# Two cross-attention layers on one core: the values of layer 0 one product later on the tensor engine

## The chip, the cores and the metric

The kernel runs on one core of a Trainium2 chip. The time is the device time of one execution in microseconds. Three runs of the kernel before gave a median of 1915.06 us (1913.88 to 1915.12).

## The reference, cut to what matters

Two attention layers follow each other on 4 batches of 1024 tokens of width 1024, with a context of only 64 tokens for each batch. All is in float32.

```python
# layer 0: 32 query heads of 32, 8 key heads, additive mask, residual, layer norm
q = x @ Wq + bq;  k = ctx @ Wk + bk;  v = ctx @ Wv + bv
attn = softmax(q k^T / sqrt(32) + mask)          # per head, over 64 keys
x1 = layernorm((attn v) @ Wo + bo + x) * gamma + beta
# layer 1: 16 heads of 64 over layernorm(ctx), boolean mask, gated residual
y = x1 + tanh(gate) * (softmax((x1 @ Wq.T) (a @ Wk.T)^T / 8) (a @ Wv.T)) @ Wo.T
```

## The kernel before

**Blocks, subtiles, pairs.** The 4096 tokens are cut into 4 blocks of 1024, 32 subtiles of 128 (numbered t = 0 to 31) and 16 pairs of subtiles. Large products are made by a scheme with seven half-size products in place of eight (the names S1 to S4, T1 to T3, X, V, W belong to it); sums of operands for it are made on VectorE.

**The stages.** (1) Up to some 230 us: the context's keys and values, and the queries of block 0. (2) From some 230 to 600 us: `mix(t)` (L771) interleaves the attention of layer 0 of subtile t with the query products of the next block, which come out of a generator `work` (L962). (3) From some 600 to 717 us: the last 8 subtiles are mixed with `folded_queries` (L887), small products that fold layer 1's query weights with its keys (called heads below), and at the end with four steps of the first output product. (4) From then on the output product of layer 0 and all of layer 1, pair by pair. Stages 2 and 3 are what the change touches.

**One subtile of layer 0.** `attend0` (L654) makes the scores in two fronts (L680): 8 small TensorE products each into a PSUM tile `big`, which VectorE copies out with the mask added (L684). VectorE takes the maxima (L691); ScalarE takes the exponentials: 24 of the 32 heads one by one (L698), each with its sum, the other 8 together (L706), while VectorE subtracts and sums for those (L694, L711). Then VectorE inverts the sums (L712) and divides (L715) in two halves, `divide(1)` and `divide(0)`. For t below 19 (`by_turning`) the probabilities are transposed through DRAM: GpSimd's queue writes them out (L735, `p<-s`) and reads them back by quarters (L739, four transfers `pq<-p`, one buffer), and VectorE turns them with two stream transposes (L419) into two tiles `pT`; this is called the flip. From t = 19 on TensorE transposes (L407) and ScalarE copies out (L410 and L414). The **values** of a subtile (L759) are 16 small products of `pT` with the value matrix, shown as x16 by the trace; they need both flips. ScalarE copies their PSUM tile to `oT` (L398, L400) and issues its DMA (L765). For t below 19 values use the pool `big`, of two buffers, which the fronts use too; later values, heads, ScalarE's transposes and the query products share the pool `wx`, of four banks.

**The order.** `mix(t)` issues front 0, a place for other work, front 1, maxima and exponentials, a second and a third place, then the values of subtile t-2 (from t = 20 on those of t-1, whose flip is issued a little earlier), total and divide of half 1, a fourth place, the flip of t-1, total and divide of half 0, the transfers of the flip of t, and a fifth place. `other()` fills a place with one step of `work` as long as the subtile's count lasts. The count is 3 at even and 4 at odd t up to 15 and from 24 on, and 3 from 16 to 23, so that **the fourth place holds a step only at odd t up to 15 and at t = 25, 27, 29, 31**, and the fifth never holds one. In stage 2 a step is a product of queries, four matrix products of 128x512 (x8 in the trace, L576); in stage 3 it is one group of heads (L897, x8), or at t = 30 and 31 a product with Wo (L446). The layer that records the program may move instructions within an engine's list where data allow it, so an engine's list follows this order only roughly; each engine then works its own list in order.

**What waits on what around it.** Half 1's total and division do not depend on the values. The flip of t-1 writes into the two `pT` tiles that the values of t-2 read. The `big` buffer that the values fill is taken again by front 1 of subtile t+1, so ScalarE has to have copied it out by then. ScalarE's copy of `oT` stands among the exponentials of subtile t in its list.

Of the kernel before, what the change touches and what calls it, by code (L numbers as in the profile page):

```python
# [71 lines left out]
def tile_two_cross_attentions(  # L72
# [150 lines left out]
    for i in range(2):  # L223
        t = scratch.tile([P, H], F32, tag="cnat", name=f"ctx_{i}", bufs=2)
# [3 lines left out]
    for w, n in ((wk0, "wk0"), (wv0, "wv0")):  # L228
        t = wpool.tile([P, KC, 256], F32, tag="wb", name=n)
# [408 lines left out]
    def by_turning(t):  # L638


        return t < NSUB - SUB - 5
# [3 lines left out]
    def load_queries(t):  # L645
        q = qpool.tile([P, KC, P], F32, tag="q", name=f"q0_{t}")
        nc.sync.dma_start(out=q, in_=qTd[t // SUB][:, :, sub_ap(t % SUB)])

        m = small.tile([P, 2, S], F32, tag="m0", name=f"m0_{t}", bufs=2)
        for e in range(2):  # L650
            nc.sync.dma_start(out=m[:, e], in_=mask0[sub_ap(t), :])
        queries[t] = q, m
# [75 lines left out]
    def outputs0(t):  # L728

        b = t * P // L  # L730
        s = probs.pop(t)
        pTs = {}
        if by_turning(t):

            nc.gpsimd.dma_start(out=p0[t], in_=s)  # L735
            pq = pqpool.tile([P, NQ, 512], F32, tag="pq", name=f"pq0_{t}")
            v = p0[t].rearrange("(u i) (a w) -> a i u w", i=Q, a=NQ)
            for a in range(NQ):
                nc.gpsimd.dma_start(out=pq[a * Q : (a + 1) * Q], in_=v[a])  # L739

        def flip(c):
            pT = pTs[c] = ppool.tile([P, 8, P], F32, tag="pT", name=f"pT0_{t}_{c}")
            if by_turning(t):
                turn_quarters(pq, pT, (c * 8, (c + 1) * 8))
                return

            turn(s[:, c * 1024 : (c + 1) * 1024], pT, t >= NSUB - SUB)

        def values():
            oT = opool.tile([P, KC, P], F32, tag="oT", name=f"oT0_{t}")  # L750
            ps = big() if by_turning(t) else [wx(), wx()]


            for c in range(2):
                for i in range(2):
                    for e in range(2):
                        bank = ps[:, e * 512 : (e + 1) * 512] if by_turning(t) else ps[e]
                        on, at = slice(e * S, (e + 1) * S), (2 * c + i) * 32
                        nc.tensor.matmul(  # L759
                            bank[at : at + 32], v0[on, b, c, i, :],  # L760
                            pTs[c][on, i * 4 : (i + 1) * 4].rearrange("p g l -> p (g l)"),
                            start=True, stop=True, tile_position=(e * S, at),
                        )
            copy_out(oT.rearrange("p g l -> p (g l)"), ps)
            nc.scalar.dma_start(out=oTd[t // 2][:, :, sub_ap(t % 2)], in_=oT)  # L765

        return flip, values

    turned = {}

    def mix(t, count):  # L771


        front, largest, exps, total, divide = attend0(t)
        places = 5

        def other():
            nonlocal count, places
            for _ in range(-(-count // places)):
                next(work)  # L780
                count -= 1
            places -= 1

        def powers(n):
            for _ in range(n):
                if exps:
                    exps.pop(0)()

        def values(u):
            if u in turned:  # L790
                turned.pop(u)[1]()

        def flip(u):
            for c in range(2):
                turned[u][0](c)

        front(0)
        if (t + 1) % SUB:
            load_queries(t + 1)
        other()  # L800
        front(1)
        largest(0)
        powers(1)
        largest(1)
        powers(1)
        other()
        plain = t and not by_turning(t - 1)
        if plain and t - 2 not in turned:
            flip(t - 1)
        powers(1)  # L810
        other()
        powers(2)
        if t - 2 in turned:
            values(t - 2)
            if plain:
                flip(t - 1)
        total(1)
        divide(1)
        if plain:
            values(t - 1)  # L820
        other()
        if t and not plain:
            flip(t - 1)
        powers(len(exps))
        total(0)
        divide(0)
        turned[t] = outputs0(t)
        other()
# [195 lines left out]
    for t in range(last):  # L1024
        n = 28 - AHEAD if t // SUB == NBLK - 2 else 28
        mix(t, (t % SUB + 1) * n // SUB - t % SUB * n // SUB)
    go_on(FOLD_AHEAD)
    n = 4 * KC - FOLD_AHEAD + FIRST
    for i in range(SUB):
        mix(last + i, (i + 1) * n // SUB - i * n // SUB)  # L1030
# [38 lines left out]
    def turn_x1(pair, xq, pool=None, tag="xT"):  # L1069

        xT = (pool or xTpool).tile([P, KC, 2 * P], F32, tag=tag, name=f"xT_{pair}")

        def half(h):
            turn_quarters(xq, xT[:, h * HK : (h + 1) * HK, :], (h * HK, (h + 1) * HK))

        def blocks():
            lefts[pair] = left_out(xT, lpool if pool else lxpool, f"x_{pair}")

        return [lambda: half(0), lambda: half(1), blocks]
# [4 lines left out]
    flip, values = turned.pop(NSUB - 1)  # L1084
# [13 lines left out]
    for pair in range(1, NPAIR):  # L1098
# [30 lines left out]
        if pair == NPAIR - 2:  # L1129
            xq = load_x1(0)  # L1130
            turned = turn_x1(0, xq, o2pool, "o2")
# [165 lines left out]
```

## Time and profile before

| what | us |
|---|---|
| median of 3 runs | 1915.06 |
| the profiled execution | 1915.11 |
| its span on the core | 1913.3 |
| TensorE (PE) busy in the span | 1868.9 |
| VectorE (DVE) busy | 1292.1 |
| ScalarE (ACT) busy | 427.9 |
| GpSimd (POOL) busy | 179.1 |
| PE busy from 230 to 545 us (315 us) | 308.53 |
| PE busy from 600 to 720 us (120 us) | 106.05 |
| PE busy from 1200 to 1800 us, each 100 us | 100.00 |

The profile describes one execution, from the first instruction to the last. A table of stretches gives the busy time of each engine in a window, with the clock that TensorE was granted (1.00 is full) and the share of the DMA engines' time in use. A timeline row has the start, the length, the engine, the line, the operation, its output and input, the number of merged instructions, and in brackets how long the engine had stood idle before it and what released it. A matmul that has begun counts as busy, even where the next instruction of its merged row waits; so a row that is longer than its kind hides a wait too.

### The profile page before, as it was taken

The numbers are of one execution on the slowest core, as the hardware profiler recorded it, in microseconds if no ns is written. First come the engines' busy times: TensorE is split into PE (matmuls) and PEld (weight loads), VectorE is DVE, ScalarE is ACT, GpSimd is POOL, SyncE is SP. The second block draws the span as 40 slices with busy tenths as digits, with TensorE's granted clock in tenths as the row PEclk, the third lists the DMA queues.
The fourth block names the chain that finished last, engine by engine and source line by source line (L and its number), as shares of the span: only waits on it lengthen the run. The fifth ranks groups of instructions, "written<-read, shape, count | busy, mean of one in ns | idle before, by whom it ended". The sixth has DMA issues, their size and how long they took to land.

```text
span 1913.3 us, 17522 instructions
## 1 busy us (share of the span) xinstructions
PE 1868.9 (98%) x6096; PEld 880.0 (46%) x6096; DVE 1292.1 (68%) x1582; ACT 427.9 (22%) x1396; POOL 179.1 (9%) x212
## 2 busy tenths in 40 slices
PE   8999999999998899999999999999999999999999
PEld 7744444444455653343344444444444444444444
DVE  3425589789878985575568778557665766576653
ACT  1101575666536751212100001000000000000000
POOL 0016011111100103121113100000000000000000
PEclk9999999999999899999999999999999999999999
DMA  8996599899878966567473363466656565657421
GB/s 276 184 222 192 158 253 247 253 252 261 252 186 275 302 234 207 188 207 238 164 218 138 121 141 90 110 165 158 150 143 165 150 158 143 165 142 165 121 88 44
DMA packets 220745, 350.54 MB, mean 183 GB/s; under 512 B 26992, under 2 KB 146160, under 8 KB 215664
## 3 DMA queue, kind: packets, MB, share of 16 engines
q1 hardware_dynamic: 152896, 242.44, 45.8%
q0 software_dynamic: 15216, 60.83, 10.5%
q10 hardware_dynamic: 52544, 46.14, 8.8%
q8 instruction: 48, 0.79, 0.2%
q14 instruction: 41, 0.34, 0.1%
HBM read 207.53 MB, written 141.82 MB: 183 GB/s over the span
## 4 chain that ended last, share of the span: by engine, by line
PE 82%; DVE 8%; DMA 5%; issue 2%; ACT 2%; POOL 0%; SPq 0%; DVEq 0%; POOLq 0%; ACTq 0%
PE wx L446 59%; PE wx L576 14%; PE big L680 2%; DMA pq<-p 2%; PE big L924 1%; PE wx L379 1%; PE big L379 1%; DVE s L684 1%; PE big L759 1%; DMA p<-s 1%; DMA q<-qTd 1%; DVE s L715 1%; DVE mx L691 1%; DVE sm L711 1%; DMA o<-oTd 1%
## 5 line engine op out<-in xcount | busy, mean ns | idle before, releaser
L455 DVE TENSOR_TENSOR r<-wx,r 128x512 f32<-128x512 f32 x224 | 153.5, 686 | 230.1 <-PE wx L446 215.3
L698 ACT ACTIVATE s<-s,mx 128x64 f32<-128x64 f32 x488 | 162.8, 335 | 74.9 <-DVE mx L691 70.7
L502 ACT ACTIVATE s<-s 128x1024 f32<-128x1024 f32 x32 | 33.7, 1057 | 651.7 <-DVE s L501 651.7
L459 DVE TENSOR_TENSOR s<-wx,key_bias 128x512 f32<-128x512 f32 x64 | 44.1, 690 | 136.7 <-PE wx L446 136.7
L446 PE MATMUL wx<-wo_B,S 128*128 128x512 f32 x256 | 117.1, 600 | 1.5 <-DVE r L455 1.5
L576 PE MATMUL wx<-xT,wq_S 128*128 128x512 f32 x256 | 116.5, 598 | 0.8 <-ACT z L587 0.8
L446 PE MATMUL wx<-b_B,pT 128*128 128x512 f32 x256 | 115.8, 593 | 0.6 <-ACT pT L414 0.6
L446 PE MATMUL wx<-b_B,S_p 128*128 128x512 f32 x256 | 116.0, 596 | 0.0
L446 PE MATMUL wx<-a_B,xT 128*128 128x512 f32 x256 | 115.4, 592 | 0.0
L446 PE MATMUL wx<-a_B,S_x 128*128 128x512 f32 x256 | 115.3, 593 | 0.1
L576 PE MATMUL wx<-xB,wq_A 128*128 128x512 f32 x256 | 115.1, 597 | 0.0
L446 PE MATMUL wx<-wo_B,o 128*128 128x512 f32 x256 | 114.8, 596 | 0.0
L958 POOL TENSOR_TENSOR r<-r,bo 128x1024 f32<-128x1024 f32 x30 | 78.5, 2625 | 313.8 <-DMA r<-in_x_dram 159.4
L684 DVE TENSOR_TENSOR s<-big,m 128x1024 f32<-128x1024 f32 x64 | 77.4, 1215 | 28.4 <-PE big L680 26.8
L680 PEld LDWEIGHTS big<-kv,q 64*128 64x128 f32 x1024 | 71.1, 195 | 48.3 <-issue 39.9
L698 ACT ACTIVATION_READ_ACCUMULATOR s<-s,mx 128x1 f32 x488 | 91.4, 187 | 0.0
L680 PE MATMUL big<-kv,q 64*128 64x128 f32 x1024 | 82.6, 292 | 2.6 <-DMA q<-qTd 2.6
L419 DVE STREAM_TRANSPOSE pT<-pq 128x1024 f32<-128x1024 f32 x66 | 78.0, 1219 | 3.3 <-DMA pq<-p 3.3
L446 PEld LDWEIGHTS wx<-wo_B,S 128*128 128x128 f32 x256 | 47.1, 190 | 67.7 <-issue 51.2
L715 DVE TENSOR_TENSOR s<-s,sm 128x1024 f32<-128x1024 f32 x64 | 77.0, 1216 | 0.9
L446 PEld LDWEIGHTS wx<-wo_B,o 128*128 128x128 f32 x256 | 47.8, 190 | 63.5 <-issue 62.3
L446 PEld LDWEIGHTS wx<-a_B,S_x 128*128 128x128 f32 x256 | 48.5, 190 | 62.0 <-issue 58.4
(162 smaller groups left out, 2903.5 us busy)
## 6 DMA issues: line engine op xcount, KB each, us to landing
p<-s POOLq DMA_DIRECT2D x19, 1024.0 KB, 8.1
pq<-p POOLq DMA_DIRECT2D x76, 256.0 KB, 6.0
xq<-in_x_dram SPq DMA_DIRECT2D x64, 256.0 KB, 10.2
q<-qTd SPq DMA_DIRECT2D x32, 512.0 KB, 7.4
oTd<-oT ACTq DMA_DIRECT2D x32, 512.0 KB, 7.4
ad<-a POOLq DMA_DIRECT2D x16, 1024.0 KB, 8.9
o<-oTd SPq DMA_DIRECT2D x16, 1024.0 KB, 5.1
r<-in_x_dram SPq DMA_DIRECT2D x32, 512.0 KB, 5.3
```

Source lines behind the costliest of these rows:

```text
L379: nc.tensor.matmul(ps[:, 0:256], w[k // HK, c // HK][:, k % HK, sub_ap(c % HK)], ct[:, k, :], start=(k == 0), stop=(k == KC - 1),)
L419: return nc.vector.transpose(dst.rearrange("p k (u i) -> p k u i", i=Q), t[:, :, k0 * Q : k1 * Q].rearrange("p u (k j) -> p k u j", j=Q),)
L446: nc.tensor.matmul(banks[name], a[s][:, k, :], w[m][:, k, :], start=first and k == 0, stop=last and k == HK - 1, skip_group_check=True,)
L455: nc.vector.tensor_tensor(at, bank, at, ALU.add)
L459: nc.vector.tensor_tensor(at, bank.rearrange("p (h s) -> p h s", s=S), bias.unsqueeze(1).to_broadcast([P, 512 // S, S]), ALU.add,)
L502: nc.scalar.activation(s, s, AF.Exp)
L576: nc.tensor.matmul(bank, w_q[a][:, k, sub_ap(i)], rows[b][:, k, :], start=first and k == 0, stop=last and k == HK - 1, skip_group_check=True,)
L680: nc.tensor.matmul(ps[:, at : at + P], q[on, c * 4 + g, :], k0bd[on, b, c, :], start=True, stop=True,)
L684: nc.vector.tensor_tensor(quarters[:, :, c * 8 : (c + 1) * 8], ps.rearrange("p (k a l) -> p a k l", a=NQ, l=Q), mask.rearrange("p e (h l) ...
L698: nc.scalar.activation(heads[:, e, k], heads[:, e, k], AF.Exp, bias=mx[:, e, k : k + 1], accum_out=sm[:, e, k : k + 1],)
L715: nc.vector.tensor_tensor(heads[:, e], heads[:, e], wide(sm[:, e]), ALU.mult)
L958: nc.gpsimd.tensor_tensor(ru, ru, bo_sb, ALU.add)
```

## The change

The values of subtile t-2 (or t-1) are issued after the fourth place and no longer before total and divide of half 1; these, and the step of the fourth place, now come first. Only at t = 20, where two sets of values fall together, does one of them stay in front.

```diff
         powers(2)
-        if t - 2 in turned:
+        late = t - 2 in turned
+        if late and plain:
             values(t - 2)
-            if plain:
-                flip(t - 1)
+            flip(t - 1)
         total(1)
         divide(1)
+        other()
         if plain:
             values(t - 1)
-        other()
+        elif late:
+            values(t - 2)
         if t and not plain:
             flip(t - 1)
         powers(len(exps))
```

In the built program the lists differ from those before in the following. **PE:** at t = 3, 5, 7, 9, 11, 13 and 15 the values stand behind a whole product of queries that they stood in front of, or in the middle of; at t = 25, 27 and 29 behind one more group of heads and some products of the next front; at t = 31 behind one product with Wo, and the last subtile's TensorE transposes, which stood half in front of and half behind the next such product, stand together behind it. At all other t nothing moves on PE. **ACT:** at the odd t up to 15 the copy to `oT` stands behind 5 to 8 more exponentials (one to six at t = 15), mostly behind all of them; at t = 25, 27 and 29 behind two more copies of heads. **DVE:** a few neighbours change places at t = 5, 9, 13 and 15 (at 5 and 13 the last division comes in front of the turning of some input rows). **SP and POOL:** the same order.

## The prediction

> **What bounds the kernel now.** I read first the page's busy times, then the table of stretches, then the waits of PE in stage 2, then PE's and DVE's timelines. All durations are from the profiled execution, 1915.11 us with a span of 1913.3 (1.8 us lie around it); it stands 0.05 us above the median of 1915.06, so the sum is made against 1915.1.
>
> ```profile
> PE 1868.9 (98%) x6096; PEld 880.0 (46%) x6096; DVE 1292.1 (68%) x1582; ACT 427.9 (22%) x1396; POOL 179.1 (9%) x212
> ```
>
> TensorE is the bound: 98% busy. What an edit can gain is the time in which PE stands or drags: 44 us in all, and by the table of stretches these lie in few places.
>
> ```profile
> 286.80:325.40 38.60, 35.39 (x168) 15.38 (x168) 38.06 (x37) 21.12 (x101) 5.49 (x10) 0.96 0.98 256
> 325.40:389.00 63.60, 63.60 (x298) 29.27 (x290) 48.77 (x56) 43.82 (x214) 11.00 (x20) 1.00 0.89 256
> 389.00:420.90 31.90, 31.81 (x153) 14.47 (x152) 26.78 (x32) 22.11 (x107) 5.48 (x10) 1.00 1.00 257
> 420.90:459.00 38.10, 35.81 (x166) 15.50 (x170) 37.67 (x36) 22.42 (x110) 5.49 (x10) 1.00 0.88 250
> 600.00:720.00 120.00, 106.05 (x771) 71.34 (x768) 102.43 (x115) 77.61 (x181) 9.03 (x12) 0.93 0.86 290
> ```
>
> The columns after the window are its length and the busy times of PE, PE's loads, DVE, ACT and POOL, then PE's clock and the DMA share. The reader is to see two stretches of stage 2 in which DVE is full, 38.06 of 38.60 and 37.67 of 38.10 us (it turns and sums the input rows of the next block there), and PE loses 3.2 and 2.3 us; between them DVE has a quarter of its time free and PE loses nothing visible. In stage 3 PE loses most. What PE waits for in stage 2 is one thing:
>
> ```profile
> PE big L759 <- DVE pT L419: 6.2, 5, 2.1
> ```
>
> that is, the values for their flips, 6.2 us in 5 waits. The timeline shows them, and more than them: values without a wait take 1.09 us (first row below), and where the second flip comes later than the first, the row is longer by the wait inside it.
>
> ```profile
> 272.18 1.09 PE L759 MATMUL big<-pT,kv 64*32 64x512 f32 x16
> ...
> 282.55 3.60 PE L576 MATMUL wx<-xT,wq_S 128*128 128x512 f32 x8
> 288.24 2.96 PE L759 MATMUL big<-pT,kv 64*32 64x512 f32 x16 [2.09 <-DVE pT L419]
> 291.13 3.95 PE L576 MATMUL wx<-xT,wq_A 128*128 128x512 f32 x8
> ```
> ```profile
> 307.89 1.35 PE L759 MATMUL big<-pT,kv 64*32 64x512 f32 x16
> ...
> 323.89 2.10 PE L759 MATMUL big<-pT,kv 64*32 64x512 f32 x16 [1.78 <-DVE pT L419]
> 325.92 3.70 PE L576 MATMUL wx<-xB,wq_A 128*128 128x512 f32 x8
> ```
>
> **Part 1, stage 2: values behind one product (3.6 us) at odd t.** The wait before plus the row's excess over 1.09 is, at t = 3, 5, 7, 9, 11, 13, 15: 0.77 (row of 1.86 at 253.9), 2.09 + 1.87 = 3.96, 1.78 + 1.01 = 2.79, 0.70 (1.79 at 356.3), 0, 1.47 + 1.01 = 2.48 (422.3) and 0.48 + 1.01 = 1.49 (457.6). Together 12.2 us. A product that stands ready runs in that time; each sum is near or below 3.6 us, so at the place itself all of it goes. That is the upper bound of the gain. What decides is the next subtile, where no product moves. PE then asks for the flip of t-1 earlier; does it come earlier? The flips of subtiles 3, 4 and 5 on DVE:
>
> ```profile
> 286.85 2.37 DVE L419 STREAM_TRANSPOSE pT<-pq 128x1024 f32<-128x1024 f32 x2 [2.37 <-DMA pq<-p]
> ...
> 305.76 2.36 DVE L419 STREAM_TRANSPOSE pT<-pq 128x1024 f32<-128x1024 f32 x2
> ...
> 322.51 2.36 DVE L419 STREAM_TRANSPOSE pT<-pq 128x1024 f32<-128x1024 f32 x2
> ```
>
> The first waits for its DMA, not for PE; after it DVE has no gap but 0.42 us until 324.8. So at **t = 5** the 3.96 are gained and at **t = 6** they are given back: PE, earlier by 0.77 + 3.96, has done its products at 304.4 (in the old run's times; the last of them still waits for a DVE addition at about 300.8), while the second flip ends at about 307.6 against 308.1 before. Values of 4 end at about 308.4 in place of 309.2. I keep 0.77 up to here. At **t = 7** the flip of 5 stays where DVE puts it, 322.5 to 324.9; the moved product fills that time, the values run at 325.1 without a wait, and the 2.79 are kept, if the following stretch lets PE be ahead: there DVE is 77% busy and waits itself for PE (1.27 and 1.22 us for the fronts of subtile 8), so it follows. At **t = 9** 0.70 more is kept. At **t = 13** the same as at 5 happens: the flip of 11 waits 0.89 us for its DMA, then DVE is full to 459, so the 2.48 come back as a wait at **t = 14** (its values already wait 0.43 + 1.01). At **t = 15** 1.49 are kept, since the full stretch ends there. Sum kept: 0.77 + 2.79 + 0.70 + 1.49 = 5.75.
>
> **Covers.** ScalarE's copy to `oT` now stands behind up to 8 more exponentials of 0.33 us, 2.7 us. It has to be done by front 1 of the next subtile, which stands 4.8 us behind the end of the values (a front of 1.1, a product of 3.6). At t = 5 the exponentials would end at 291.3, the copy (0.99) at 292.3, front 1 stands at 295.5: hidden. At t = 7 it is tight, 330.6 against 331. If the cover is gone, at most 2.7 us less what PE gained. In return ScalarE no longer stands in front of the copy, 11.4 us in 5 times before, with exponentials queued behind it. The flip of t-1 needs the values of t-2 done; DVE comes to it some 15 us later, so nothing. The divisions ahead of the values: the same DVE work in nearly the same list, 0; at t = 5 and 13 the division of half 0 is some 1 us earlier and a front's copy 1 us later, which I set against each other. SP's and POOL's lists keep their order; 0.
>
> **Part 2, stage 3: values behind one more group of heads.** At t = 25:
>
> ```profile
> 620.83 1.13 PE L897 MATMUL wx<-kT,wq1T 64*128 64x256 f32 x4 [0.47 <-ACT pT L410]
> 621.88 1.09 PE L759 MATMUL wx<-pT,kv 64*32 64x512 f32 x16
> 622.90 0.49 PE L680 MATMUL big<-kv,q 64*128 64x128 f32 x4
> 623.96 1.40 PE L897 MATMUL wx<-kT,wq1T 64*128 64x256 f32 x7 [0.57 <-ACT a L903]
> ```
>
> Here values start at once, and the group behind them waits 0.57 us for a bank that ScalarE frees at L903. The banks go round: with the order changed, the moved group finds its banks free, and it is the values that need the two banks of the group before, both copied out only at 624.4, behind an exponential of 1.8 us. PE then has 1.06 (heads) + 0.4 (fronts) to do from 621.9, stands some 1.0 us in place of 0.57, and reaches the next transposes some 0.3 us later. DVE sets the pace of these subtiles (some 11.9 us each, of which 11.4 are DVE work), so the true cost lies between 0 and 0.45; I take 0.3 each for t = 25 and 29. At t = 27 DVE stands 1.40 us for the load of `o` and adds four sums of 0.7; PE has time, 0. At t = 31 the transposes of the last subtile stand together: the second half needs banks that the copies of the first half (0.5 each) free, between 0 and 1.1 us; nearest is one copy with its start-up, 0.7. Part 2 costs 1.3, with bounds of 0 and 2.5.
>
> **Sum.** 1915.1 - 5.75 + 1.3 = **1910.7 us**, 0.23% under the median. By the bounds: from 1902.9 (all of 12.2, nothing lost) upwards.
>
> **The clock.** Where PE has stood long, it then drags. The group of heads that takes 1.06 us took 1.98 at 612.9, and a front of 1.09 took 1.74 at 614.6, after waits of 2.05 and 2.55 us; 1.6 us were lost in one such stretch. At 288.2, after 2.09 us, the same shows (values 2.96, then a product of 3.95 in place of 3.70), after 1.78 us at 323.9 it does not. The limit lies near 2 us in this trace. [...]
>
> **Rivals.** *All of the waits go* (1915.1 - 12.2 + 1.3 = 1904.2): DVE's full stretches would have to start earlier with PE. For it: they start at a DMA whose chain starts at a division that PE's fronts release. Against it: the DMA share of 0.96 (230 to 286.8 us) and 1.00 ahead of them, and that inside them DVE has nothing to give. *DVE or the DMA chain sets the pace throughout*: each wait comes back one subtile later, the gains are nil, and stage 3 costs up to 1.3: 1915.1 to 1916.4. For it: DVE is at 85% over stage 2, and each flip hangs on two DMAs with 8 us and 6 us to landing. Against it: no wait for values at t = 8, 10, 12. *The clock* (slower): the wait returned at t = 6 and t = 14 is 2.1 us or more, and those of about 1 us in stage 3 join others there; from some 2 us in a stretch on, each brings 1.6 us of half clock. Four such, 6.4, with 1.3 of part 2, and only the gains at t = 3, 9 and 15 left (2.96, if the drag eats those of t = 7): 1915.1 + 6.4 + 1.3 - 2.96 = 1919.8. Against it: the old run has one such stretch in stage 2, which the change removes from t = 5. That the change does nothing is excluded for 11 of 32 subtiles by the lists.
>
> **Chances.** Forecast 0.45 (1908.5 to 1912.7), all waits 0.17, no gain 0.20, clock 0.18. A measurement of this kernel can tell some 0.2% from no change, 3.8 us: 1911.2 is the border, two thirds of the forecast's case lie below it. Faster 0.17 + 0.33 = 0.50; same 0.12 + 0.18 = 0.30; slower 0.18 + 0.02 = 0.20. The range that leaves out 2 in 10 takes in the middle of the first rival and all of the second and stops short of most of the third: 1904.0 to 1917.5.
>
> **What would show it.** Right: no wait in front of the values at t = 5, 7, 13, 15; PE at its front of subtile 8 some 3.5 us earlier than at 330.4; waits of 2 us or more at the values of t = 6 and 14. Wrong: the values of t = 7 wait in spite of the product (then DVE runs later than I hold); front 1 waits for the copy to `oT`; PE's clock below 0.96 in the two full stretches, or below 0.93 from 600 to 720; stage 3 longer by more than 2.5 us.

## The result, and the profile after

The changed kernel takes 1909.5 us (median of 8 runs, 1906.8 to 1911.4), the kernel before 1913.8 us beside it (8 runs, 1911.8 to 1915.6): ratio 0.9974, with a 95% interval of 0.9966 to 0.9983 (the two medians alone, divided, give 0.9977). Run once more with other kernels (e11 below) the ratio is 0.9959 (0.9943 to 0.9974). The forecast, 1910.7 of 1915.1, is a ratio of 0.9977. The gain is 0.26%, more than the 0.2% that can be told from no change, though the first interval reaches down to 0.17%.

The profiled execution took 1911.4 us with a span of 1909.7, 3.6 us less than before. The busy times:

```profile
PE 1865.5 (98%) x6096; PEld 879.6 (46%) x6096; DVE 1290.2 (68%) x1582; ACT 427.4 (22%) x1396; POOL 178.5 (9%) x212
```

The counts of instructions are the same, and TensorE is the bound as before. What PE waits for from 230 to 545 us:

```profile
PE big L759 <- DVE pT L419: 4.1, 2, 2.1
PE wx L576 <- DVE u L593: 1.1, 2, 0.8
PE big L680 <- DMA q<-qTd: 0.4, 1, 0.4
```

Five waits for flips have become two, and two kinds have come that the old list did not have. PE's timeline from t = 5 to t = 8 shows where (start, length, operation, and in brackets the idle time ahead of it with what ended it):

```profile
284.58 3.60 PE L576 MATMUL wx<-xT,wq_A 128*128 128x512 f32 x8
288.11 1.09 PE L759 MATMUL big<-pT,kv 64*32 64x512 f32 x16
...
299.40 3.70 PE L576 MATMUL wx<-xN,wq_A 128*128 128x512 f32 x8 [0.76 <-DVE u L593]
305.23 2.10 PE L759 MATMUL big<-pT,kv 64*32 64x512 f32 x16 [2.13 <-DVE pT L419]
...
313.07 10.57 PE L576 MATMUL wx<-xB,wq_A 128*128 128x512 f32 x24
323.57 1.09 PE L759 MATMUL big<-pT,kv 64*32 64x512 f32 x16
324.59 1.12 PE L576 MATMUL wx<-xT,wq_S 128*128 128x512 f32 x2
326.13 1.16 PE L680 MATMUL big<-kv,q 64*128 64x128 f32 x16 [0.41 <-DMA q<-qTd]
```

At t = 5 and t = 7 the values (288.11 and 323.57) stand behind the product and start at once, in 1.09 us. At t = 6 they wait 2.13 us, and their row is 2.10 long because the second flip comes late too. The front of t = 8, at 330.41 before, comes at 326.13, after a wait of 0.41 us for its own load. The flips of subtiles 3, 4 and 5 on VectorE:

```profile
285.49 2.37 DVE L419 STREAM_TRANSPOSE pT<-pq 128x1024 f32<-128x1024 f32 x2 [2.42 <-DMA pq<-p]
...
303.85 2.36 DVE L419 STREAM_TRANSPOSE pT<-pq 128x1024 f32<-128x1024 f32 x2
...
320.60 2.36 DVE L419 STREAM_TRANSPOSE pT<-pq 128x1024 f32<-128x1024 f32 x2
```

They start 1.4, 1.9 and 1.9 us earlier than before: VectorE's full stretch follows its first load, not PE, which is 5.9 us ahead at the front of t = 6. In the table of stretches (length, busy PE, PEld, DVE, ACT, POOL, PE's clock, DMA share, GB/s) VectorE is still full in the first of these rows:

```profile
286.80:325.40 38.60, 35.71 (x174) 15.41 (x172) 38.09 (x38) 21.41 (x105) 6.70 (x13) 1.00 0.96 254
...
420.90:459.00 38.10, 35.76 (x165) 16.11 (x162) 37.15 (x37) 22.52 (x105) 5.88 (x12) 1.00 0.88 273
600.00:720.00 120.00, 105.80 (x730) 68.49 (x730) 100.26 (x114) 74.44 (x171) 11.26 (x13) 0.91 0.84 285
```

Where the time came from, by the same instructions' starts in the two profiles (us, gained at the place; a minus is given back):

| at t = | 3 | 5 | 6 | 7 | 8 | 9 | 10 to 12 | 13 | 14 | 15 | to the end of stage 2 | sum |
|---|---|---|---|---|---|---|---|---|---|---|---|---|
| forecast | 0.77 | 3.96 | -3.96 | 2.79 | 0 | 0.70 | 0 | 2.48 | -2.48 | 1.49 | 0 | 5.75 |
| measured | 0.97 | 4.49 | -3.98 | 2.37 | -1.02 | 0.90 | 0.19 | 2.75 | -2.17 | 1.75 | -0.12 | 6.13 |

The row at t = 7 includes the wait of 0.41 us in front of t = 8; the 1.02 at t = 8 are the row of its values, 2.10 us long in place of 1.09. PE enters stage 2 0.4 us earlier, which is scatter, leaves it 6.6 us earlier and is still 6.4 us ahead at the last values of stage 3. Some 3 us of that go near 717 us. PE, VectorE and GpSimd there:

```profile
720.14 5.40 PE L446 MATMUL wx<-wo_T,S 128*128 128x512 f32 x8 [2.24 <-DVE r L455]
```
```profile
719.39 0.69 DVE L455 TENSOR_TENSOR r<-wx,r 128x512 f32<-128x512 f32 x1 [3.07 <-POOL r L962]
```
```profile
717.02 6.95 POOL L962 TENSOR_TENSOR r<-r,bo 128x1024 f32<-128x1024 f32 x3 [34.03 <-DMA r<-in_x_dram]
```

GpSimd adds `bo` to rows that have just landed, VectorE's addition waits for it, PE waits 2.24 us for VectorE (0.97 before) and then needs 5.40 us for a product of 3.70. Whether that belongs to the change is a question for the runs.

### The profile page after: what moved, and what is told of

Its sections match the earlier page's. It is cut to its first block, busy times and chain, and to the rows that moved or that the text cites. A ratio compares the mean times of both kernels' runs of the same rounds, so it can differ in the third digit from the quotient of the medians.

```text
span 1909.7 us, 17518 instructions
## 1 busy us (share of the span) xinstructions
PE 1865.5 (98%) x6096; PEld 879.6 (46%) x6096; DVE 1290.2 (68%) x1582; ACT 427.4 (22%) x1396; POOL 178.5 (9%) x212
## 4 chain that ended last, share of the span: by engine, by line
PE 80%; DVE 9%; DMA 5%; ACT 3%; issue 2%; POOL 0%; SPq 0%; DVEq 0%; ACTq 0%; POOLq 0%
PE wx L446 59%; PE wx L576 12%; ACT s L698 2%; PE big L680 2%; DVE s L684 2%; PE wx L379 1%; PE big L379 1%; PE big L928 1%; DVE mx L691 1%; DVE s L715 1%; DMA q<-qTd 1%; DMA pq<-p 1%; DMA p<-s 1%; PE big L759 1%; DVE sm L711 1%
## 5 line engine op out<-in xcount | busy, mean ns | idle before, releaser
L299 ACT ACTIVATE rstd<-rstd 128x1 f32<-128x1 f32 x32 | 6.5, 203 | 316.1 <-DVE rstd L298 316.1
```

## The experiments

**Theory.** A product in front of the values fills the wait at odd t; where VectorE's full stretch goes on, the next subtile hands the gain back; stage 3 costs little. **Rivals:** the gain comes from elsewhere (stage 3, the divisions); or what hands the gain back is not VectorE's work but the loads.

### Which stage: e1 and e2

e1 keeps the old order from t = 20 on, e2 keeps it up to t = 19. Against the changed kernel, e1 reads

```diff
-        other()
         if plain:
             values(t - 1)
-        elif late:
+        other()
+        if late and not plain:
             values(t - 2)
```
For e1 was expected:

> The values one product later up to t = 19 only, stage 3 as before. My theory (the gain is PE's removed waits for flips in stage 2, and stage 3 costs or brings nearly nothing): 3.5 to 5.5 us under the kernel before, as the whole change. Rival (the gain, or a loss that hides a larger one, lies in stage 3 or in where the slow-clock stretches fall there): less than 2 or more than 6.5 us under it.

and for e2:

> The values later at t = 25, 27, 29, 31 only. My theory: within 1.5 us of the kernel before (I had priced it at +1.3; the changed kernel's trace shows PE no later at the end of stage 3 than at its start). Rival: 3 us or more under it.

e1: 1909.0 us, ratio 0.9973 (0.9963 to 0.9983). e2: 1915.9 us, 1.0005 (0.9996 to 1.0014). The whole gain is stage 2's; stage 3 costs 1.0 us, with an interval of -0.8 to 2.7, so it cannot be told from nothing.

### Which subtiles: e3 and e4

e3 moves the values only at t = 5 and 13, the places said to be handed back; e4 at all the others of stage 2. The edit is `moved = t in (5, 13)`, or the rest, added to the condition.

> The values later at t = 5 and 13 only, the two places with the longest waits (3.96 and 2.48 us), where VectorE is full behind them. My theory: the time gained there is given back one subtile later, so 0 to 1.5 us under the kernel before, with PE some 4 us ahead at the front of subtile 6 and less than 1 us ahead at the front of subtile 7. Rival (what counts is the sum of waits removed, wherever): 6.4 of 12.2 us removed, so half of the whole change or more, 2.5 us and more under it.

> The values later at t = 3, 7, 9, 11 and 15, not at 5 and 13 and not in stage 3. My theory: 3.5 to 5.5 us under the kernel before, all that the whole change brings, though only 5.75 of 12.2 us of waits are removed. Rival (the sum of waits counts): half of the whole change, 2 to 2.5 us under it.

e3: 1912.7 us, 0.9988 (0.9979 to 0.9997); e4: 1909.8 us, 0.9977 (0.9963 to 0.9990). In e3 6.4 us of waits go at t = 5 and 13, and the waits at t = 6 and 14 stand there at 2.12 and 2.00 us; 1.5 us are left in its profile between the values of 0 and of 18, and 4.4 in e4's, of 6.1 in the changed kernel's. By the ratio e3 gains 2.3 us (0.6 to 4.0), between what the theory and the rival allowed it. So t = 5 and 13 are mostly returned, not wholly, and the other five places carry most of the gain.

### The divisions: e5

Moving the two divisions ahead of the values, without the product, was not run: in the built program it leaves the lists of all five engines as they were. e5 asks the other half: the product alone.

```diff
-        total(1)
-        divide(1)
         other()
         if plain:
             values(t - 1)
         elif late:
             values(t - 2)
+        total(1)
+        divide(1)
```

> The product stands in front of the moved values as in the changed kernel, but the divisions stand behind the values again. With the old order of the product, moving the divisions alone leaves the instruction list of every engine as it was, so the question is only whether they matter beside the moved product. Theory (the time comes from the product alone, and VectorE divides at its own pace): the values of t = 5, 7, 13, 15 start without a wait, the waits at t = 6 and 14 are 2.0 to 2.2 us, and the time is that of the changed kernel, 1909.5 us, within 1.5; ratio to before 0.997 to 0.9985. Rival (the divisions in front are what keeps the quotients early enough for the next subtile): the waits at the flips or fronts behind grow by 1 us at five to ten places, 1913 to 1916 us, ratio 0.9995 to 1.001.

e5: 1910.2 us, 0.9982 (0.9973 to 0.9990). The waits at t = 6 and 14 are 2.13 and 1.71 us as the theory has it, but two rows differ: at t = 5 the row of the values is 1.96 long, and at t = 16 they wait 1.87 us. In the traces the lists of e5 and of the changed kernel differ in stage 2 only on VectorE, near 255 us (t = 3) and from 385 to 393 us (t = 11), so no other order stands directly behind those two rows; at t = 16 a wait of 0.51 us stands in e4 too. The intervals overlap with the changed kernel's, so whether the divisions in front are worth about a microsecond beside the product stays open.

### What hands the gain back: e6, e9, e12

e6 lets the last three of the four sums over the next block's rows (2.27 us each on VectorE) run in the first steps of the next block, e9 puts the second sum (L184) on GpSimd:

```diff
-            run(sums[1:])
+            if not spread:
+                run(sums[1:])
...
-            fills = {}
+            fills = dict(enumerate(later))
```
```diff
+        def tt(out, a, b, op, n):
+            return (nc.gpsimd if n in moved else nc.vector).tensor_tensor(out, a, b, op)
...
-                rows, fills = rows0(blk + 1)
+                rows, fills = rows0(blk + 1, (1,))
```

> The changed kernel, and the last three of VectorE's sums over the next block's input rows run in the first three steps of the next block, not at the end of the old one's; so VectorE's full stretches (near t = 4 to 6 and t = 12 to 14) lose some 8 us of work. Theory (a full VectorE is what hands the waits on from t = 5 to 6 and from 13 to 14): the waits at t = 6 and 14 fall from 2.13 and 2.00 us to under 0.7, with them the slow stretch of the values' row goes (2.10 us back to near 1.1), and stage 2 ends 1.5 to 4 us earlier than in the changed kernel: 1905.5 to 1908 us, ratio 0.9955 to 0.997. Rival (the flips there hang on their loads, not on VectorE): the waits stay at 1.8 us or more, and the sums are merely late for the next block's first products: 1909 to 1913 us, ratio 0.9975 to 0.9995.

> The changed kernel, and the second of the four sums over the next block's input rows (L184, 2.27 us on VectorE, in front of the flip that the values at t = 6 and t = 14 wait for) runs on GpSimd. Theory (VectorE's amount of work in the full stretch hands the waits on to t = 6 and 14): that flip comes 2.3 us earlier, the wait of 2.13 us at t = 6 falls under 0.3 us and that of 2.00 us at t = 14 likewise, and the time falls by 1 to 4 us under the changed kernel's: ratio to before 0.9955 to 0.997. Rival (the sum of about 6.5 us on GpSimd delays the loads that GpSimd issues for the flips, or slows VectorE beside it): the wait at t = 6 stays at 1.5 us or more or comes back at t = 7 or t = 8, ratio 0.9975 to 1.001.

e6: 1919.5 us, 1.0026 (1.0014 to 1.0038); e9: 1919.1 us, 1.0019 (1.0006 to 1.0031). Both are slower than the kernel before. The sum that e9 moved takes 4.54 us on GpSimd there (at 299.64 us), where 6.5 was expected, an estimate (GpSimd's additions of half that width take 2.34 to 3.34 us in the changed kernel); VectorE's rows beside it, a front's copy of 1.20 and a flip of 2.36 us, are as long as in the changed kernel (1.21 and 2.36). PE's waits in stage 2 of e6:

```profile
PE big L681 <- DMA q<-qTd: 8.1, 1, 8.1
PE big L760 <- DVE pT L419: 3.7, 3, 2.5
PE wx L577 <- DVE u L594: 0.9, 1, 0.9
```

The wait at t = 6 did fall, from 2.13 to 1.06 us (1.05 in e9), though not under the 0.7 us (0.3 in e9) that were expected; at t = 14 it did not (2.49 and 2.22). VectorE's rows ahead of the flip of 4, in the changed kernel and in e6, show why:

```profile
299.27 2.27 DVE L184 TENSOR_TENSOR xT<-xB,xT 128x2048 f32<-128x2048 f32 x1
...
302.71 1.22 DVE L691 TENSOR_REDUCE mx<-s 128x16 f32<-128x1024 f32 x1
303.85 2.36 DVE L419 STREAM_TRANSPOSE pT<-pq 128x1024 f32<-128x1024 f32 x2
```
```profile
302.17 2.35 DVE L692 TENSOR_REDUCE mx<-s 128x16 f32<-128x1024 f32 x2
304.43 2.36 DVE L419 STREAM_TRANSPOSE pT<-pq 128x1024 f32<-128x1024 f32 x2
```

The sum of 2.27 us left the place, and a second maxima instruction of 1.1 us came into it. From the flip of 3 to that of 4 VectorE took 17.29 us in e6 and in e9, against 18.36 in the changed kernel, without a gap in any of them: 1.07 us less, and the wait fell by 1.07 and 1.08. At t = 14 a second maxima instruction and a subtraction came in front of the flip: from the flip of 11 to that of 12 it took 17.47 us in e6 and 18.45 in e9, against 17.69, again without a gap. So there the edits took little or nothing off VectorE's work, and did not test it; besides, the flip of 11 waited 1.49 and 2.68 us for its load, against 0.82.

The front of t = 8 now waits 8.1 us (5.1 in e9) for its queries. SP's queue in the changed kernel and in e6:

```profile
312.94 0.34 SPq L590 DMA_DIRECT2D qTd<-z  x1
313.33 8.06 SPq L651 DMA_DIRECT2D m<-in_mask_dram  x4
321.50 0.65 SPq L647 DMA_DIRECT2D q<-qTd  x1
324.16 0.33 SPq L590 DMA_DIRECT2D qTd<-e  x1
```
```profile
309.35 1.63 SPq L652 DMA_DIRECT2D m<-in_mask_dram  x2
319.54 0.33 SPq L591 DMA_DIRECT2D qTd<-e  x1
325.88 1.25 SPq L648 DMA_DIRECT2D q<-qTd  x2
```

In e6 the load of the queries stands behind the store of the next block's first piece `e`, which waits for VectorE, and comes out 4.4 us later, 1.5 of which is a later start of the stage. e12 puts that store on GpSimd's queue, to see whether this place was the whole loss. Beside the edit of e6:

```diff
+            queue = nc.gpsimd if name == "e" and i == 0 else nc.sync
-            nc.sync.dma_start(out=qTd[blk][:, h * HK + i, u * HT : (u + 1) * HT], in_=kept[i][name])
+            queue.dma_start(out=qTd[blk][:, h * HK + i, u * HT : (u + 1) * HT], in_=kept[i][name])
```

> The changed kernel with the three sums spread over the next block's first steps, as in the run before that did so, and with the store of a block's first two query pieces `e` on GpSimd's queue in place of SP's. In the two runs that took work off VectorE in front of the flip, SP's list had that store, which waits for the next block's first addition near 319 us, in front of the load of the queries of t = 8; the load came out at 325.88 and 324.34 us in place of 321.50, and TensorE waited 8.1 and 5.1 us for it. Here the load stands in front again. Theory (that place in the queue was the whole loss of those runs, and VectorE's amount of work still hands the waits on): the front of t = 8 waits 2 us or less, the wait at t = 6 is 1.1 us as there, and the ratio to before is 0.9945 to 0.9975. Rival (the queries' way through memory, or VectorE's later list, takes back whatever the flip gains): 4 us or more at the front of t = 8 or in the flips behind it, ratio 0.999 to 1.003.

e12: 1920.6 us, 1.0025 (1.0016 to 1.0035). My theory fell. The load stands in front again and the front waits longer, 9.2 us. SP's queue in e12, and what SP waited for:

```profile
306.78 16.21 SPq L653 DMA_DIRECT2D m<-in_mask_dram  x4
323.16 1.24 SPq L649 DMA_DIRECT2D q<-qTd  x2
```
```profile
SPq L653 <- DMA oTd<-oT: 8.7, 1, 8.7
```

The mask loads ahead of the queries wait for the landing of a store of `oT`, which ScalarE issued behind the values of t = 6. The same wait, of 3.4 us, stands in the changed kernel (3.9 before), and e6's own profile had it already, directly at the load of the queries:

```profile
SPq L648 <- DMA oTd<-oT: 5.9, 1, 5.9
```

The store of `e` had gone out at 319.54 us, the load at 325.88: it was held by the landing of `oT` (3.8 us in e9), not by the store that e12 moved. That landing took 14.9 us from the issue in e6, 14.3 in e9 and 14.7 in e12, against 9.2 in the changed kernel, though the store was issued earlier (310.9, 309.9 and 307.9 us, against 311.8). The first load of the queries itself then took 8.9, 6.0 and 9.8 us to land, against 4.5. Why these transfers took longer stays open. What is shown: in e6 and e9 1.07 us less VectorE work ahead of the flip shortened the wait at t = 6 by 1.07 and 1.08 us, and the queries of t = 8, with waits of 8.1 and 5.1 us, then ended the gain. Whether the freed time would be kept if that load came early stays open; no run here had both.

### The loss near 717 us: e7, e8, e10, e11

e7 adds `bo` to the rows of pair 1 on VectorE; e8 asks for the sums of `o`, for whose load VectorE stands near t = 27, one chunk later; e10 has both, and e11 is the changed kernel again.

```diff
-                nc.gpsimd.tensor_tensor(ru, ru, bo_sb, ALU.add)
+                (nc.vector if pair == 1 else nc.gpsimd).tensor_tensor(ru, ru, bo_sb, ALU.add)
...
+            if k == 6:
                 a = left_out(o, early, "0_0")
```

> The changed kernel, with the two additions of bo to the rows of pair 1 on VectorE in place of GpSimd. Theory (of the 6.1 us that stage 2 gives, about 3 are lost again near 717 us, where VectorE's first addition of the product waits 3.07 us for GpSimd's 6.95 us of additions and TensorE 2.24 us behind it, and then runs at half its clock): the wait and the slow product (5.40 in place of 3.70 us) go, 1906 to 1908 us, ratio 0.9955 to 0.997. Rival (the loads of these rows are late, whoever adds, or VectorE has no room there): TensorE waits as long for the same addition, and the time stays at 1909 to 1911 us, ratio 0.997 to 0.9985.

> The changed kernel, with VectorE's sums over the first half of o asked for one chunk later in stage 3 (after chunk 6, not 5). Theory (VectorE stands for the load of o near t = 27 with everything else queued behind it, TensorE waits 3.1 to 6.0 us for the flip there, and the half clock follows): the wait at t = 27 falls under 1.5 us, and one or two of the stretches at half clock go: 1904 to 1907.5 us, ratio 0.995 to 0.9968. Rival (stage 3 is paced by VectorE's amount of work, and the sums only move the wait to a later subtile, at worst in front of the first product of the last stage): the time stays within 1.5 us of 1909.5, or rises to 1913, ratio 0.997 to 0.9995.

> The changed kernel with both of the earlier edits: bo added on VectorE for pair 1, and the sums of the first half of o asked for one chunk later. Theory (the first takes away the wait near 717 us, 1 to 3 us in a single execution, and the second only moves a wait): near 1908 us, ratio 0.9962 to 0.9976. Rival (what the profile shows near 717 us differs from run to run and is filled by other waits in most executions): as the changed kernel alone, ratio 0.997 to 0.998.

> The changed kernel once more, to see how far its own profile and time move from execution to execution. Theory: stage 2 shows the same waits at t = 6 and 14 (2.1 and 2.0 us) and stage 3 another set of stretches at half clock; the ratio to before is 0.9966 to 0.9983, and the wait near 717 us is 1.0 us or less (the rows' landing was late by chance in the first profile). Rival (the wait near 717 us belongs to the change): 2 us or more there again.

e7: 1908.2 us, 0.9969 (0.9957 to 0.9981). e8: 1909.6, 0.9975 (0.9967 to 0.9984). e10: 1909.6, 0.9963 (0.9950 to 0.9976). e11: 1909.0, 0.9959 (0.9943 to 0.9974). In e7 PE has no wait near 717 us, but the time cannot be told from the changed kernel's, and in e10 a wait of 1.30 us stands there in spite of the same edit. e8 tests nothing: its built lists are those of the changed kernel on all five engines, so asking later moved no instruction, and e8 is the changed kernel once more (VectorE's wait for `o` is 1.84 us in it, 1.59 in the first profile; PE's wait behind it at t = 27 is 4.68 and 3.41). In the same way e10 is e7 once more, and the 1.30 us near 717 us that e10 has and e7 has not is a difference between two executions. Whether the sums of `o`, asked for later, would help stays untested. e11 settles 717 us:

```profile
717.20 3.70 PE L446 MATMUL wx<-wo_T,S 128*128 128x512 f32 x8 [0.98 <-DVE r L455]
```

0.98 us, as before (0.97), and no slow product; in e8 it is 0.95 us. The loss in the first profile was of that execution, not of the change. No version here beats the changed kernel by more than the runs can tell.

The profiles side by side, cut at the start of the values of 0, 18 and 31 (us):

| profile | stage 2 to there, 0 to 18 | 18 to 31 | 31 to the end |
|---|---|---|---|
| before; e2 (old order in stage 2) | 301.1; 301.4 | 174.3; 173.9 | 1198.0; 1198.2 |
| changed; e11; e1 (same order in stage 2) | 294.9; 294.6; 294.7 | 174.4; 172.9; 174.0 | 1200.8; 1197.2; 1198.8 |
| e8; e7; e10 (the same list of PE in stage 2) | 295.7; 297.6; 297.8 | 173.4; 174.6; 174.7 | 1197.4; 1196.0; 1197.4 |
| e3; e4 | 299.5; 296.7 | 172.2; 175.7 | 1197.8; 1196.9 |
| e5; e6; e9; e12 | 297.7; 304.5; 302.2; 306.4 | 174.5; 175.1; 174.3; 175.6 | 1198.6; 1197.0; 1198.8; 1198.4 |

The first column shows the change, 6.1 to 6.8 us between the first two rows, and what t = 14 and t = 8 take back in e7 and e10; the other two scatter by 3.5 and 4.8 us whatever the order. The whole time fell by less than the first column, 5.0 us by the ratio of 0.9974 and 4.3 by the medians; a cost of 1 us in stage 3 would fit between, but that scatter hides it.

## Why the prediction was right, step by step

- **Waits at odd t go: right.** None is left at t = 5, 7, 13 and 15, and each place gave within 0.6 us of its term. The term of 3.96 at t = 5 was not all wait: a row whose second flip comes late takes 2.10 us at full clock (422.28 before), so 0.86 of the row of 2.96 was half clock, which began at 288.3 us.
- **t = 5 and 13 come back at t = 6 and 14: right,** 3.98 and 2.17 us, as waits of 2.13 and 2.00 us with rows of 2.10. The reason given, VectorE's fullness, holds for t = 6, where e6 and e9 took 1.07 us off its work and the wait fell by as much; at t = 14 VectorE has no gap either, but no run took work off it there, so the cause is read from the trace and not shown by a run. The step also had the flip of 4 come only 0.5 us earlier; it came 1.9 us earlier (0.4 of it the earlier start), so that 0.5 us of t = 5 was kept.
- **t = 7 is kept: right, at 2.37 for 2.79.** What the step left out is the front of t = 8. It was said to come 3.5 us earlier and came 4.3 us earlier, and that is where its queries land: 0.41 us of wait here, which is what 2.37 lacks to 2.79, 1.17 in e11, 1.87 in e10. The values of t = 8 gave back 1.02 us more (2.10 for 1.09, not so in e11): their flip waited 1.70 us for its own load, where it waited for none before. The load of the queries comes out only 2.4 us earlier than before (321.50 for 323.89). "SP's and POOL's lists keep their order; 0" was true of the order and not of the cost: the list that stayed as it was became the limit at t = 8, where PE came 4.3 us earlier and the load 2.4.
- **Covers: right.** Front 1 waits nowhere for the copy to `oT`; ScalarE stands 7.9 us in 3 waits ahead of that copy, where it was 11.4 in 5.
- **Stage 3 at 1.3 us: not refuted, and not measured.** e2 has 1.0 (-0.8 to 2.7), which holds nothing as well as the 1.3, and the profiles show no difference beyond their scatter. The mechanism is seen: the values of t = 25 now wait 0.60 us for a bank that ScalarE frees at L907.
- **The sum: in part luck.** Stage 2 gave 6.13 for 5.75 because what was kept beyond the forecast (0.51 at t = 5 and 6, 0.58 at t = 13 and 14, and smaller terms, 1.9 in all) and what was lost at t = 7 and 8 (0.42 and 1.02) and behind t = 15 nearly cancel.
- **All of the waits go** (1904.2): refuted by the two waits that stayed; the queries of t = 8 would stop it too. **No gain:** refuted by e1 and by t = 7. **The clock:** neither wait returned brought half clock in the profiles of the changed kernel; in e7 and e10 the wait of 2.00 us at t = 14 did, 2 of the 7 profiles that have this wait. So this rival is real for single executions and too rare to decide the median. One sign that was to show the forecast wrong did appear and was badly chosen: the clock of stage 3 at 0.91, below 0.93. The same window reads 0.94 in e11 and 0.91 in e4, whose stage 3 has the old order.
- The wait that decides the half clock was put at "near 2 us". That step failed: see the last section.

## What to carry to other kernels

The wait at t = 5, which VectorE's pace set, was mostly moved by filling it: 4.49 us were gained there and 3.98 given back at t = 6. So ask, for each place, whether the late engine has room before the next time it is needed, and count only what is kept there. When the bound engine gets ahead, look at every queue whose list does not change: here PE came to the front of t = 8 4.3 us earlier, SP's load of its queries came out only 2.4 us earlier, and PE waited 0.41 us for it (1.87 in e10). Before moving an entry of a queue, read what that queue waits for at the late entry itself: e6's own profile named it, 5.9 us for the landing of `oT`. And compare the lists of an edit with those before it; an edit that leaves them alike, as e8's did, is the same kernel once more. A single profile's stretch of 3 us outside the changed stage is no evidence until a second profile of the same kernel shows it.

## What the runs showed of the hardware

In these runs the half clock went by a grid in time, and by the work in one cell of it more than by the length of a wait. In each of the 14 profiles the starts of the stretches at half clock lie apart by whole multiples of 3.413 us (in the changed kernel 601.5, 639.1, 656.2, 666.4 and 721.0: 11, 5, 3 and 16 of them), and each lasts 3.41 us or a multiple, but for the last (2.83 us in the changed kernel, 2.36 in the kernel before), which ends behind the program's last instruction. PE's busy time in the cells of that grid around the wait of t = 14, in the changed kernel and in e7 (cell, length, busy PE, clock, DMA share, GB/s):

```profile
434.29:437.70 3.41, 2.17 (x18) 1.00 0.99 384
437.70:441.12 3.42, 3.42 (x22) 1.00 0.83 254
```
```profile
433.97:437.39 3.42, 1.42 (x10) 1.00 0.98 355
437.39:440.80 3.41, 3.41 (x22) 0.50 0.51 156
```

The wait is 2.00 us in both. In the changed kernel a border of the grid cuts it, the cell keeps 2.17 us of work and the clock stays; in e7 it lies whole in one cell, 1.42 us of work are left, and the next cell runs at half. Of the cells at full clock between 255 and 735 us, all 38 with less than 1.45 us of work were followed by a cell at half clock; from 1.45 to 2.2 us it was 12 of 44, and above that 7 more ran at half, all after 590 us. So a wait of 2.49 us at t = 14 of e6 cost no clock and a wait of 1.87 us at t = 8 of e10 did. That fits the stretches of stage 3, which lie elsewhere in each profile of the same order (the first from 600 us on at 601.5 us in the changed kernel, 606.2 in e8 and 605.4 in e11); no run set the grid's place on purpose.
